# A pair's first products and tanh issued one pair ahead in the mixing of a graph layer

## The chip, the cores and the metric

The kernel runs on one core of a Trainium2 chip. The metric is the device time of one execution in microseconds (us). TensorE (PE) multiplies matrices into PSUM, VectorE (DVE) and GpSimd (POOL) do elementwise work, ScalarE (ACT) does activations such as tanh, and SyncE (SP) issues most of the transfers. The engines run side by side and wait for each other by semaphores; each takes its own instructions in order.

## The reference

The network has four graph layers over 8 batches of 2048 nodes with 64 features. Each layer is `x = x + layer(relu(layernorm(x)))`. The change lies in the end of layer 0, which mixes two candidates per node, `industry` (a product with the adjacency matrix) and `g` (from the hyperedges):

```
def attn_scores(f):
    return jnp.tanh(f @ fcW + fcb) @ av
...
pair = jnp.stack([industry, g], axis=2)
coefs2 = jax.nn.softmax(attn_scores(pair), axis=-1)
out = jnp.einsum('bnk,bnkf->bnf', coefs2, pair)
```

A softmax over two values needs only the difference of the two scores, and the weight of one is half of one plus the tanh of half that difference. The kernel uses this: with d the difference of the two scores, the mix is half of `(industry + g) + (industry - g) * tanh(d / 2)`.

## The kernel before, in words

Features lie on the partitions. Two batches of 64 features fill the 128 partitions, so the 8 batches are 4 pairs, numbered q = 0 to 3. The 2048 nodes are cut in 4 chunks of 512. The function `mix` loops over the chunks and in each over the pairs, 16 turns in all. In the text a pair is named by its q, and a mark as in 0' means the chunk after.

One turn of the loop, for a pair of a chunk:

- For each of the two sources, `ind` and then `g`: two half products with the weights `fcw`, one for each batch (64 partitions each), into a PSUM tile `p1` of two banks (two such tiles exist), and one tanh on ACT over both halves (L658). A tile counts as two half products; each shows as two records in the trace. The trace writes `p` for p1.
- `dt` on POOL is the difference of the two tanh (L660), with two buffers.
- Two products with `av` on PE turn dt into the score `pd`, one PSUM bank. Its tanh, `t2`, is on ACT (L668).
- `total` on POOL is the sum of the two sources (L666).
- On DVE come the mixing operations: `df` = ind - g (L670), times t2 (L671), plus total (L672), and half of it added to `x` (L673).

After the four pairs of a chunk, x is stored (L241), and the layer norm of the next layer is made for that chunk by a generator, `norm_parts`. Its first part centres x on PE (`center`), squares on ACT (L264), takes the relu on ACT or DVE (L269, L267), sums the squares by a product (`to_rows`), and makes the standard deviation: a square root on ACT (L272) and a reciprocal on DVE (L273). Its second part spreads the result by four products (`from_rows`), one for each pair, and DVE multiplies and writes it into two tiles for each pair (L634). These PSUM banks are the three of `bank`. The two parts run at the end of the turns q = 0 and q = 1 of the following chunk. ACT loads a table for the square root and another one for the return to tanh.

At the end of the turn q = 2, `each` brings the next chunk's `g`: four gathers by index on POOL's queue (L750), four tiles of four transposes on PE through `bank` (L756), and copies shared between ACT and DVE (L172, L174).

The order of the code is not the order of the engines. When the program is built, a planner places the instructions of each engine, and the pools decide with their buffers what has to wait. So the trace shows products of the next pair ahead of pd of a pair, although the code names them after it.

Of the kernel before, what the change touches and what calls it, by code (L numbers as in the profile page):

```python
# [7 lines left out]
F = mybir.dt.float32  # L8
# [4 lines left out]
AF = mybir.ActivationFunctionType  # L13
# [6 lines left out]
P = 128  # L20
NB = 8
N = 2048
D = 64
NP = NB // 2
NT = N // P
R = P // NP
CW = 512
NC = N // CW
# [99 lines left out]
class Kernel:  # L128
# [490 lines left out]
    def mix(self, slots, ind, g, fcw, av, each=None):  # L619


        nc, tc = self.nc, self.tc
        big = [slots.tile([P, 2, NP, CW], F, name=f"mix{i}", tag=f"q{6 + i}") for i in range(3)]
        ring = slots.tile([P, 4, 2, CW], F, name="tanh", tag="q9")

        end = [slots.tile([P, 2, NP, CW], F, name=f"end{i}", tag=f"q{4 + i}") for i in range(2)]
        end = end[0][:, 0], end[0][:, 1], end[1][:, 0]
        xe, xo = self.chebyshev(slots)

        def write(q, ch, xr, scale):  # L630
            s = slice(ch * CW, (ch + 1) * CW)
            for i, dst in enumerate((xe, xo)):
                h = slice(i * D, (i + 1) * D)
                nc.vector.tensor_mul(dst(q)[h, s], xr[h], scale[h])  # L634


        with (
            tc.tile_pool(reuse_waits="tile", name="mix", bufs=2) as w,
            tc.tile_pool(reuse_waits="tile", name="mix_ps", bufs=1, space=PSUM) as ps,
        ):  # L640
            def bank():
                return ps.tile([P, CW], F, name="bank", bufs=3)

            norm = iter(())
            if each is not None:
                each(0, bank)
            for ch in range(NC):
                s = slice(ch * CW, (ch + 1) * CW)
                x, sq, xr = end if ch == NC - 1 else (b[:, ch % 2] for b in big)
                nc.sync.dma_start(x, self.xs[0][ch])  # L650
                for q in range(NP):
                    th = [ring[:, 2 * (q % 2) + i] for i in range(2)]
                    for i, src in enumerate((ind, g)):
                        p1 = ps.tile([P, 2, CW], F, name="p1", bufs=2)
                        for half in range(2):
                            h = slice(half * D, (half + 1) * D)
                            self.mm(p1[:, half], fcw[h], src(q)[h, s])
                        nc.scalar.activation(th[i], p1, AF.Tanh, bias=self.col("fcb"))  # L658
                    dt = w.tile([P, 2, CW], F, name="dt")
                    nc.gpsimd.tensor_sub(dt, th[0], th[1])  # L660
                    pd = ps.tile([P, CW], F, name="pd")
                    for half in range(2):
                        self.mm(pd[half * D : (half + 1) * D], av[:, :D], dt[:, half])

                    total = w.tile([P, CW], F, name="total")
                    nc.gpsimd.tensor_add(total, ind(q)[:, s], g(q)[:, s])  # L666
                    t2 = w.tile([P, CW], F, name="t2")
                    nc.scalar.activation(t2, pd, AF.Tanh, scale=0.5)  # L668
                    df = w.tile([P, CW], F, name="df")
                    nc.vector.tensor_sub(df, ind(q)[:, s], g(q)[:, s])  # L670
                    nc.vector.tensor_mul(df, df, t2)  # L671
                    nc.vector.tensor_add(df, df, total)  # L672
                    nc.vector.scalar_tensor_tensor(  # L673
                        x[:, q], df, 0.5, x[:, q], op0=OP.mult, op1=OP.add
                    )
                    if q < 2:
                        next(norm, None)
                    elif q == 2 and each is not None and ch + 1 < NC:
                        each(ch + 1, bank)
                self.store_x(0, ch, x)  # L680
                std = w.tile([P, CW], F, name="std")
                norm = self.norm_parts(ch, x, xr, sq, std, bank, write)
            for _ in norm:
                pass
# [1037 lines left out]
    def attend(self, ih, b, tiles, w, ps, num, den, h1, rows, ed, ed2, shift):  # L1722


        nc, ident = self.nc, self.ident
        HALF = N // 2
        q, s = b // 2, b % 2
        pe = ps.tile([P, HALF], F, name="pe")
        for c in range(2):
            self.mm(  # L1730
                pe[:, c * CW : (c + 1) * CW],
                ident[: 2 * NB, b : b + 1].to_broadcast([2 * NB, P]),
                rows[:, ih * HALF + c * CW : ih * HALF + (c + 1) * CW],
            )
        es = w.tile([P, HALF], F, name="es")
        nc.scalar.copy(es, pe)
        acc = ps.tile([P, HALF], F, name="acc")
        for jt in range(NT):
            m = w.tile([P, HALF], F, name="m", bufs=5)
            e = ed[:, jt, b : b + 1]  # L1740

            t = w.tile([P, HALF], F, name="t")
            nc.gpsimd.tensor_scalar(t, es, 0.2, ed2[:, jt, b : b + 1], op0=OP.mult, op1=OP.add)
            nc.vector.scalar_tensor_tensor(m, es, e, t, op0=OP.add, op1=OP.max)
            nc.vector.tensor_mul(m, m, tiles[jt])
            nc.scalar.activation(m, m, AF.Exp, bias=shift[:, b : b + 1])
            for c in range(2):
                self.mm(
                    acc[:, c * CW : (c + 1) * CW],
                    h1[:, jt, q, s * D : s * D + P], m[:, c * CW : (c + 1) * CW],  # L1750
                    start=jt == 0, stop=jt == NT - 1,
                )
        own, other = slice(s * D, (s + 1) * D), slice((1 - s) * D, (2 - s) * D)
        nc.scalar.copy(num[own], acc[own])
        nc.scalar.copy(den[own], acc[other])
# [595 lines left out]
```

## Time and profile before

| | us |
|---|---|
| median of 3 runs | 2163.15 |
| lowest and highest | 2158.54, 2169.57 |
| the profiled execution, its own time | 2161.53 |
| its span | 2159.8 |
| first tanh of the mixing, L658 | starts at 467.9 |
| last L673 | starts at 617.3 |
| reciprocals of the four norms, L273 | start at 513.76, 553.86, 592.46, 623.49 |
| 32 tanh, L658 | 1.11 each |
| 16 dt, L660 | 2.34 to 2.80 each |
| 16 total, L666 | 1.26 to 1.77 each |
| 16 t2, L668 | 0.60 each |
| 16 L670 | 0.68 to 3.12 each |

The span is the time from the first to the last instruction of the profiled execution; its own time has 1.73 us around it. Positions on the time axis count from the start of the span. In the lines of the page and of the tables by stretches, an engine is followed by its busy time and, after an x, the number of its instructions. In the list of waits stand the engine and the line that waited, what it waited for, the total of it, how often, and the longest one. In the timeline stand the start, the duration, the engine, the line and the operation, and in brackets the idle time before it with what ended it. All products of the helper `mm` have the line L166 and are told apart by their tiles. PE counts as busy also when its clock is low.

### The profile page before, as it was taken

How to read it: one execution, taken by the hardware profiler on the slowest of the kernel's cores; microseconds unless marked ns; L12 is line 12 of the kernel's file. 1: busy time of each engine (PE TensorE's matmuls, PEld its weight loads, DVE VectorE, ACT ScalarE, POOL GpSimd, SP SyncE). 2: the span in 40 equal slices, each digit the busy share in tenths (PEclk: the TensorE clock that was granted, in tenths of full speed). 3: DMA queues.
4: the chain of work that ended last, by engine and by line, in shares of the span. 5: the costliest groups of instructions: out<-in, count | busy, mean ns of one | idle time of the engine just before them, and what ended most of it. 6: DMA issues, size and time to landing. Idle time of an engine off the chain costs nothing. (4 is left out here: it accounts for less than half of the span.)

```text
span 2159.8 us, 21301 instructions
## 1 busy us (share of the span) xinstructions
PE 1945.0 (90%) x7466; PEld 1163.0 (54%) x7466; DVE 1133.9 (53%) x1956; ACT 712.2 (33%) x1343; POOL 706.0 (33%) x595
## 2 busy tenths in 40 slices
PE   5879999978879999999999998899999999669885
PEld 1425766642237774353453543677777666445433
DVE  7877677736661123425434255698703222248774
ACT  6412555534543440020110201324335333248400
POOL 0000467754310005707447166011000000177870
PEclk8868999987769999999999999999999999879997
DMA  8230333441024460050230500556444444375665
GB/s 318 82 109 6 103 104 116 134 166 39 40 80 126 123 175 31 5 151 1 73 83 0 122 1 28 169 176 223 167 125 129 135 149 147 132 221 166 177 184 183
DMA packets 108796, 253.64 MB, mean 117 GB/s; under 512 B 20912, under 2 KB 21056, under 8 KB 101376
## 3 DMA queue, kind: packets, MB, share of 16 engines
q1 hardware_dynamic: 89264, 181.45, 27.0%
q0 software_dynamic: 17104, 66.47, 10.1%
q10 hardware_dynamic: 2304, 4.20, 0.5%
q8 instruction: 62, 1.02, 0.2%
q14 instruction: 62, 0.51, 0.1%
HBM read 218.30 MB, written 33.78 MB: 117 GB/s over the span
## 5 line engine op out<-in xcount | busy, mean ns | idle before, releaser
L325 ACT CAST adj<-adj_t 128x512 fp32r<-128x512 f32 x384 | 237.4, 619 | 687.2 <-PE pp L166 354.7
L1408 POOL TENSOR_TENSOR acc<-acc,y 128x512 f32<-128x512 f32 x224 | 277.2, 1269 | 449.2 <-DVE y L1403 449.2
L166 PE MATMUL pp<-adj,hi 128*128 128x512 f32 x1280 | 365.6, 405 | 0.1
L166 PE MATMUL pk<-q,w 128*128 128x512 f32 (+1 forms) x1024 | 358.2, 611 | 4.3 <-ACT q L1376 3.0
L166 PE MATMUL pp<-adj,lo 128*128 128x512 f32 x1280 | 358.7, 400 | 0.0
L166 PEld LDWEIGHTS pp<-adj,hi 128*128 128x128 f32 x1280 | 242.1, 191 | 72.4 <-issue 16.0
L166 PEld LDWEIGHTS pp<-adj,lo 128*128 128x128 f32 x1280 | 244.0, 191 | 56.5
L166 PEld LDWEIGHTS pk<-q,w 128*128 128x128 f32 (+1 forms) x1024 | 136.5, 188 | 214.1 <-issue 167.3
L1403 DVE SCALAR_TENSOR_TENSOR y<-pk,bias,q 128x512 f32<-128x512 f32 x224 | 157.7, 746 | 142.0 <-PE pk L166 135.7
L166 PE MATMUL acc<-q,ident 128*128 128x512 f32 x416 | 202.9, 614 | 26.4 <-DVE q L2138 16.5
L2048 POOL DMA_INDIRECT ring<-f_rows,near x121 | 139.7, 1154 | 67.0 <-issue 28.0
L166 PEld LDWEIGHTS acc<-q,ident 128*128 128x128 f32 x416 | 76.7, 194 | 102.4 <-issue 47.2
L2152 POOL IOTA q<- 128x2048 int32 x1 | 1.8, 1834 | 316.5 <-PE p L166 316.5
L166 PE MATMUL pp<-adj,x_ind_hi 128*128 128x512 f32 x256 | 94.7, 486 | 2.2 <-DVE q L738 1.9
L1840 POOL TENSOR_TENSOR q<-q,beta 128x512 f32<-128x512 f32 x57 | 67.9, 1193 | 54.6 <-DVE beta L1816 30.8
L1403 DVE SCALAR_TENSOR_TENSOR acc<-pk,bias,q 128x512 f32<-128x512 f32 x32 | 22.6, 747 | 119.9 <-PE pk L166 119.9
L166 PE MATMUL bank<-std,from_rows 32*128 32x512 f32 x128 | 46.7, 894 | 41.9 <-DVE std L273 33.8
L2119 DVE TENSOR_TENSOR q<-ring,e 128x1024 f32<-128x1024 f32 x58 | 70.1, 1219 | 8.9 <-PE acc L166 8.8
L166 PE MATMUL pp<-adj,x_ind_lo 128*128 128x512 f32 x256 | 71.7, 399 | 0.0
L1530 POOL DMA_INDIRECT q<-in_adj_dram,order x15 | 19.0, 1270 | 160.3 <-DVE top L1544 133.5
L166 PEld LDWEIGHTS pp<-adj,x_ind_hi 128*128 128x128 f32 x256 | 48.5, 189 | 38.9 <-issue 23.7
L1495 DVE SCALAR_TENSOR_TENSOR q<-p,cols,q 128x512 f32<-128x512 f32 x16 | 12.0, 751 | 108.4 <-PE p L166 107.5
(411 smaller groups left out, 2768.4 us busy)
## 6 DMA issues: line engine op xcount, KB each, us to landing
adj_t<-in_adjT_dram SPq DMA_DIRECT2D x128, 512.0 KB, 4.0
adj_t<-in_adjT_dram SPq DMA_DIRECT2D x128, 256.0 KB, 3.3
rows<-in_adj_dram SPq DMA_DIRECT2D x16, 1024.0 KB, 5.6
q<-x SPq DMA_DIRECT2D x10, 1024.0 KB, 4.9
x<-q SPq DMA_DIRECT2D x9, 1024.0 KB, 3.9
q<-in_embT_dram SPq DMA_DIRECT2D x8, 1024.0 KB, 11.5
x_ch<-in_xT_dram SPq DMA_DIRECT2D x4, 1024.0 KB, 6.3
h_rows<-q SPq DMA_DIRECT2D x16, 256.0 KB, 3.6
```

Of the source, the lines that this page charges most:

```text
L166: self.nc.tensor.matmul(out, lhsT, rhs, start=start, stop=stop)
L325: nc.scalar.copy(moving, at[:, i])
L1403: nc.vector.scalar_tensor_tensor(y, pks[b, half], bias[:, b : b + 1], emb[:, b], op0=OP.add, op1=OP.mult,)
L1408: nc.gpsimd.tensor_add(acc, acc, y)
L1495: nc.vector.scalar_tensor_tensor(x[:, q], p2, self.col("b2"), x[:, q], op0=OP.add, op1=OP.add)
L1530: nc.gpsimd.indirect_dma_start(row, None, self.a["adj"], bass.IndirectOffsetOnAxis(ap=order[:, 1, t : t + 1], axis=0),)
L1840: self.nc.gpsimd.tensor_tensor(x, x, by.unsqueeze(2).to_broadcast([P, NB, D]), op=OP.mult)
L2048: self.nc.gpsimd.indirect_dma_start(to, None, self.kern.f_rows[:], bass.IndirectOffsetOnAxis(ap=index, axis=0))
L2119: nc.vector.tensor_tensor(y.rearrange("n i (b f) -> n i b f", b=NB), block[:, i : i + 2, : NB * D].rearrange("n i (b f) -> n i b f", b=NB) ...
L2152: nc.gpsimd.iota(whole, pattern=[[1, N]], base=0, channel_multiplier=0)
```

## The change

The first steps of a turn become a function, `attend`: products, tanh, dt and, now directly behind dt, total. It is called once ahead of the loop for the first pair, and then in each turn for the next pair, before the products of this pair's pd. Gathers, transposes and copies of the next chunk (`each`) move from the end of the turn q = 2 to the start of the turn q = 3, since the first pair of the next chunk is now worked on there. In the changed kernel the lines are L653 (tanh), L655 (dt), L657 (total), L681 (t2), L683 to L686 (the four mixing operations), L761 and L767 (gathers and transposes).

```diff
+            def attend(ch, q):
+                s = slice(ch * CW, (ch + 1) * CW)
+                th = [ring[:, 2 * (q % 2) + i] for i in range(2)]
+                for i, src in enumerate((ind, g)):
+                    p1 = ps.tile([P, 2, CW], F, name="p1", bufs=2)
+                    for half in range(2):
+                        h = slice(half * D, (half + 1) * D)
+                        self.mm(p1[:, half], fcw[h], src(q)[h, s])
+                    nc.scalar.activation(th[i], p1, AF.Tanh, bias=self.col("fcb"))
+                dt = w.tile([P, 2, CW], F, name="dt")
+                nc.gpsimd.tensor_sub(dt, th[0], th[1])
+                total = w.tile([P, CW], F, name="total")
+                nc.gpsimd.tensor_add(total, ind(q)[:, s], g(q)[:, s])
+                return dt, total
...
+            pairs = [(ch, q) for ch in range(NC) for q in range(NP)]
+            ahead = attend(*pairs[0])
             for ch in range(NC):
...
                 for q in range(NP):
-                    th = [ring[:, 2 * (q % 2) + i] for i in range(2)]
-                    for i, src in enumerate((ind, g)):
-                        p1 = ps.tile([P, 2, CW], F, name="p1", bufs=2)
-                        for half in range(2):
-                            h = slice(half * D, (half + 1) * D)
-                            self.mm(p1[:, half], fcw[h], src(q)[h, s])
-                        nc.scalar.activation(th[i], p1, AF.Tanh, bias=self.col("fcb"))
-                    dt = w.tile([P, 2, CW], F, name="dt")
-                    nc.gpsimd.tensor_sub(dt, th[0], th[1])
+                    dt, total = ahead
+                    if q == NP - 1 and each is not None and ch + 1 < NC:
+                        each(ch + 1, bank)
+                    if (ch, q) != pairs[-1]:
+                        ahead = attend(*pairs[NP * ch + q + 1])
                     pd = ps.tile([P, CW], F, name="pd")
                     for half in range(2):
                         self.mm(pd[half * D : (half + 1) * D], av[:, :D], dt[:, half])
 
-                    total = w.tile([P, CW], F, name="total")
-                    nc.gpsimd.tensor_add(total, ind(q)[:, s], g(q)[:, s])
                     t2 = w.tile([P, CW], F, name="t2")
...
                     if q < 2:
                         next(norm, None)
-                    elif q == 2 and each is not None and ch + 1 < NC:
-                        each(ch + 1, bank)
```

## The prediction

> **What bounds the kernel now.** The page comes first: TensorE leads, but its share is an average over stages.
>
> ```profile
> PE 1945.0 (90%) x7466; PEld 1163.0 (54%) x7466; DVE 1133.9 (53%) x1956; ACT 712.2 (33%) x1343; POOL 706.0 (33%) x595
> ```
>
> The chain that ended last names 1% of the span, so the mixing is read by itself. Its landmarks are the four reciprocals (L273) at 513.76, 553.86, 592.46 and 623.49 us. The table by stretches between them (PE, PEld, DVE, ACT, POOL, clock, DMA share, GB/s):
>
> ```profile
> 513.76:553.86 40.10, 35.53 (x90) 11.02 (x88) 27.18 (x32) 19.16 (x26) 15.76 (x8) 0.70 0.09 36
> 553.86:592.46 38.60, 33.51 (x90) 10.71 (x88) 27.19 (x33) 19.08 (x26) 15.51 (x8) 0.73 0.07 28
> 592.46:623.49 31.03, 22.98 (x54) 5.89 (x52) 17.49 (x22) 14.58 (x18) 9.21 (x7) 0.72 0.14 44
> ```
>
> DVE, ACT and POOL work 15 to 27 us of 40. PE's 35 us are at a clock of 0.70: at full clock I estimate 18 (16 half products 6.9 with twins side by side, pd 3.4, centring 3.4, to_rows and from_rows 2.0, 16 transposes 2.7). Transfers are nearly absent. So no engine is full: a chunk is a chain of waits. Who waits for whom, 473.7 to 623.5 us:
>
> ```profile
> POOL total L666 <- DVE df L672: 41.0, 9, 7.2
> ACT t L668 <- PE pd L166: 38.3, 16, 5.7
> POOL dt L660 <- ACT tanh L658: 37.6, 14, 4.5
> DVE df L671 <- ACT t L668: 37.5, 16, 8.4
> ```
>
> The last three are one loop: tanh, difference, score, tanh of half the score, mix. Each engine waits some 37 us in it. The timeline of one turn:
>
> ```profile
> 537.34 2.76 POOL L660 TENSOR_TENSOR dt<-tanh 128x1024 f32<-128x1024 f32 x1
> 537.94 2.72 DVE L670 TENSOR_TENSOR df<-q,q 128x512 f32<-128x512 f32 x1
> 540.16 1.14 PE L166 MATMUL pd<-dt,av 128*64 128x512 f32 x4 [1.78 <-POOL dt L660]
> 541.23 2.07 PE L166 MATMUL p<-q,fcw 64*128 64x512 f32 x2
> 541.36 0.60 ACT L668 ACTIVATE t<-pd 128x512 f32<-128x512 f32 x1 [3.16 <-PE pd L166]
> 543.40 1.11 ACT L658 ACTIVATE tanh<-p,cols 128x1024 f32<-128x1024 f32 x1 [1.44 <-PE p L166]
> 544.65 2.35 POOL L660 TENSOR_TENSOR dt<-tanh 128x1024 f32<-128x1024 f32 x1 [4.55 <-ACT tanh L658]
> ```
>
> PE's pd stands ahead of the last half product of the **next** pair, so the next tanh, and with it the next dt, cannot start before this dt has ended: 7.3 us from dt to dt. In the instruction order as built, three of the next pair's four products are ahead of pd already. The change moves the fourth.
>
> **What the Trainium skill says.**
> - "TensorE: Matmul & The Clock Gate", Part 1: the array runs at half or full clock, set by its activity in free-running windows of some 3.4 us. The trace agrees: a centring record is 0.43 us (504.54 to 504.97) or 0.85 (544.24 to 545.10), and the clock drops at 517.1 and 541.2, 7.06 windows apart.
> - "SBUF — State Buffer", Who interferes with whom: a VectorE operation with two SBUF inputs and a GpSimd one that reads SBUF exclude each other. It agrees: L670 at 537.94 takes 2.72 us, 0.69 alone.
> - "TensorEngine Tiling (Array Packing)", Key Properties: tiles on different rows run independently. It agrees: both halves of a p1 (4 records, 515.91) take 1.13 us, one half alone (502.95) 1.12. At half clock: 2.08 and 2.07.
>
> **The change, step by step.** Nothing is added or removed: 64 half products, 32 tanh, 16 dt, 16 total are issued as before. Costed at nothing: the gathers (L750), all 16 issued by 477.2 us and at the same place in POOL's order; the loads and stores of x, in the same order on SP; everything past the mixing, in the same order on every engine. That a later start there carries over one to one is my assumption. Moved: (a) the fourth half product to its twin's side; (b) on ACT, t2 of a pair behind **both** tanh of the next, a new wait; L671 to L673 queue behind it on DVE; (c) total directly behind its dt on POOL; its 41.0 us of waiting were no one's loss; (d) from_rows of q=3 ahead of the last half product of pair 3 and of pd of pair 2: a new wait on PE.
>
> For (b) to (d) I lay out one chunk at **full clock**, from the start of pd of pair 2 (T=0), with 0', 1', ... the next chunk's pairs. Durations: tanh 1.11, t2 0.60, dt 2.35, total 1.27, DVE operations 0.69 (0.1 between dependent ones), reciprocal 3.34, table load 1.28; p1 to its tanh 1.24, pd to t2 1.13 (501.94 to 503.07); four transposes 0.7, one after another; DVE and POOL exclude each other and take turns.
> - Tanh of (3,g) 0.2 to 1.3, t2(2) to 1.9; dt(3) 1.35 to 3.7. DVE ends the last norm's writes at 2.2, waits for the dt; mixing and copies run to 8.1.
> - PE: pd to 1.0, 12 transposes to 3.1, half of p1(0',ind) to 4.1; the fourth tile waits for a bank until 4.75, ends 5.5; the other half to 6.5, p1(0',g) to 7.4, pd(3) to 8.4.
> - Tanh(0',g) 7.75 to 8.85, t2(3) to 9.45. dt(0') 8.9 to 11.25; L671(3) 11.8; total(0') 13.1; L672(3) 13.65; dt(1') 16.0; L673(3) **16.6**.
> - DVE, behind total(1'): L670(1') 18.4, L671 and L672(0'), relu, L673(0'), relu, L670(2') to 22.7, reciprocal to **26.05** (PE and ACT have std ready at 20.95).
> - ACT: second table load to 22.25, tanh(2') to 24.4, t2(1') to 25.0. dt(2') 24.45 to 26.8, L671(1') 27.4, total(2') 28.6, L672(1') 29.2, first write, L673(1'), second write **31.3**: q=0 frees its bank, from_rows q=3 to 32.35, last half product to **33.4**, pd(2').
>
> So the period is 33.4 us at full clock, where the trace has 39.35 (mean of 40.10 and 38.60). **At half clock** the PE steps on that path cost more: 4.05 up to tanh(0',g) (pd 0.9, transposes and halves the rest), 1.9 at tanh(2'), 1.8 at the last two: **41.2**. Between them: PE stands from some 27 to 31, so T=0 finds it at half clock; pd and 12 transposes then fill a window, as the full products from 476.16 did (at full clock by 481.14). I take 0.9 for the first section and 1.8 for the last: **36.1**.
>
> First chunk: tanh(1,g) is free from tanh(0,g) at 470.8, where it had waited for pd(0); PE is continuously busy from 476.16, so clocked up: pd(2) at 484.9 (before: 492.68), reciprocal 22.7 later, 507.6 against 513.76: **-6.2**. Two chunks between: 2 x (36.1 - 39.35) = **-6.5**. End: from reciprocal 10.7 to pd(14), then 14.2 to the last one through L673(15), centring, square, to_rows, std: 24.9, and 4.1 for half clock: 29.0 against 31.03: **-2.0**. Sum **-14.7**: own time 2161.53 to 2146.8. The median of the runs is 1.6 above the profiled time, 2163.15: 2148.5, rounded to **2149**.
>
> Bounds of the unseen. Clock: all half gives start 0, 2 x (41.2 - 39.35) = +3.7, end -0.4: **+3.3**; all full gives -6.2, -11.9, -6.1: **-24**. Taking turns at the shared port: if DVE held it through L671 to L673, L673(3) ends near 14.4, but the reciprocal still ends near 26, as DVE's own list is full there: 0; if each chunk lost one more dt, +2.35 a chunk.
>
> **Rivals.**
> - *Nothing to measure*: the planner had done three quarters, and t2 behind two tanh and two table loads gives the rest back. For it: the bounds touch zero, and DVE, 27.2 of 39 us, is near full in my layout. Against: in 7.3 us from dt to dt the fourth half product is in plain sight. All steady chunks at half clock and the start's -6.2 kept: -6.2 + 3.7 - 0.4 = -2.9, 2160.
> - *Slower*: the new wait (d). PE stands behind from_rows q=3 until DVE, itself late by t2(1'), frees a bank; the idle PE stays at half clock through the next chunk, and POOL's earlier dt gets in front of L672(1') once more: 41.2 + 2.35 = 43.6, three times 4.2 over 39.35: +13, **2176**. It decides once the period exceeds 39.35. Against: the same writes took turns with mixing at 519 to 529, and PE still had work.
> - *More*: full clock throughout, -24, **2139**.
>
> **How the numbers follow.** About 0.5% (10.8 us) is what a measurement can tell from no change. The forecast, -14.7 with its own range of -8 to -20: 0.52; nothing to measure 0.27; slower 0.10; more 0.11. Faster: 0.11 and 0.44 of the forecast, 0.55; slower 0.10; same 0.35. Range: from -25, a little past all-full, to +5, past all-half: 2138 to 2168; left out are the slower rival and little else.
>
> **What would show it.** Right: reciprocals at about 507.6 and then some 36 apart; the wait of POOL's dt for tanh halved; every p1 in four-record pairs; t2 waiting on ACT's own order, not for PE; L670 to L673 longer, by waiting for POOL. Wrong: reciprocals 39 or more apart, PE idle for over 5 us before from_rows q=3, a mean clock under 0.7, or a change outside 462 to 640 us.

## The result and the profile after

The changed kernel takes 2153.12 us (median of 5 runs, 2151.85 to 2156.35), the kernel before 2163.15 (5 runs beside them). The ratio is 0.996, with a 95% interval of 0.9937 to 0.9983: some 0.4% less. The interval leaves out 1, so there is a gain, but it is smaller than the 0.5% from which the prediction would have called it one. A second set, of 13 runs, gave 0.9959 (0.9944 to 0.9974). The profiled execution has a span of 2151.4 us, where before it was 2159.8.

The page of the changed kernel, first line of its busy times, and the table by stretches between its reciprocals (span of the stretch, PE, PEld, DVE, ACT, POOL, clock, DMA share, GB/s; the first one is the end of the first chunk):

```profile
PE 1922.1 (89%) x7466; PEld 1155.0 (54%) x7466; DVE 1149.4 (53%) x1956; ACT 710.8 (33%) x1343; POOL 709.6 (33%) x595
```

```profile
475.50:514.25 38.75, 29.07 (x92) 9.73 (x92) 27.73 (x27) 18.06 (x26) 24.31 (x12) 0.87 0.17 60
514.25:553.23 38.98, 30.47 (x86) 10.34 (x86) 31.06 (x32) 18.62 (x25) 16.34 (x8) 0.78 0.10 40
553.23:591.11 37.88, 29.64 (x92) 9.69 (x89) 30.54 (x31) 18.64 (x25) 16.41 (x8) 0.86 0.07 28
591.11:618.89 27.78, 20.09 (x50) 4.68 (x46) 19.30 (x22) 12.47 (x16) 7.47 (x6) 0.82 0.15 49
```

PE does the same work of a chunk in 4 to 5 us less, and its clock is 0.78 to 0.86 and no longer 0.70 to 0.73. Some 2.6 us of this lie in the products for pd and for the banks, whose number did not change, which points to the clock; the rest lies in p1, where the clock and the placing of the halves both changed. DVE is busy 3 to 4 us **more** in a chunk, with the same instructions. The periods hardly moved: 38.98 and 37.88 us, where they were 40.10 and 38.60.

From the first tanh to the last reciprocal the mixing takes 149.46 us (469.43 to 618.89), and took 155.55 (467.94 to 623.49). This difference of -6.1 splits into -1.0 up to the first reciprocal, -1.8 over the two periods and -3.3 in the end. Outside the mixing the span differs by +1.5 before it begins and -3.8 after it ends (1532.5 us against 1536.3). The instructions there stand in the same order. In four profiles of one set below, which differ in the mixing alone, the part after it lasts from 1549.0 to 1564.2 us, so differences of this size are scatter for a single profile. But in ten of the eleven runs of the changed kernel and its variants the ratio gains more than the mixing does, by up to 9 us; whether something after the mixing gains as well was not looked into. All comparisons below use this length of the mixing beside the ratio.

Who waits for whom in the changed kernel, 475 to 615 us (total, how often, longest):

```profile
POOL dt L655 <- ACT tanh L653: 45.6, 9, 9.0
ACT tanh L653 <- PE p L166: 32.7, 12, 8.5
DVE df L684 <- ACT t L681: 23.9, 10, 8.4
POOL total L657 <- DVE df L685: 15.7, 11, 1.4
ACT t L681 <- PE pd L166: 11.3, 8, 5.3
PE bank L166 <- DVE q L634: 10.8, 3, 3.6
PE bank L166 <- DVE mix L267: 8.1, 3, 3.0
```

The loop of the view before has come apart: t2 waits 11.3 us for pd and no longer 38.3, the multiply by t2 23.9 and no longer 37.5. New are the last two rows: three times PE cannot start a from_rows before a write of the norm (L634) has freed a bank, and three times it cannot start a centring before a relu (L267) has. The first of these is also behind the second row: the wait of tanh for its products has grown from 24.3 to 32.7 us, and three of its waits, of 8.4 to 8.5 us each, end after such a from_rows.

The timeline of one turn and of the norm behind it, changed kernel:

```profile
537.50 2.35 POOL L655 TENSOR_TENSOR dt<-tanh 128x1024 f32<-128x1024 f32 x1 [1.66 <-ACT tanh L653]
537.87 2.52 DVE L684 TENSOR_TENSOR df<-df,t 128x512 f32<-128x512 f32 x1 [0.89 <-ACT t L681]
538.17 2.12 ACT L653 ACTIVATE tanh<-p,cols 128x1024 f32<-128x1024 f32 x2 [0.33 <-PE p L166]
539.90 1.08 PE L166 MATMUL pd<-dt,av 128*64 128x512 f32 x4 [0.98 <-POOL dt L655]
...
541.26 1.77 POOL L657 TENSOR_TENSOR total<-q,q 128x512 f32<-128x512 f32 x1 [1.42 <-DVE df L685]
...
543.00 2.79 POOL L655 TENSOR_TENSOR dt<-tanh 128x1024 f32<-128x1024 f32 x1
543.51 2.83 DVE L684 TENSOR_TENSOR df<-df,t 128x512 f32<-128x512 f32 x1
546.44 0.69 DVE L685 TENSOR_TENSOR df<-df,total 128x512 f32<-128x512 f32 x1
547.05 0.69 DVE L267 TENSOR_SCALAR mix<-bank 128x512 f32<-128x512 f32 x1
547.79 2.08 PE L166 MATMUL bank<-mix,center 128*128 128x512 f32 x2 [2.99 <-DVE mix L267]
549.91 0.60 ACT L264 ACTIVATE mix<-bank 128x512 f32<-128x512 f32 x1 [5.41 <-PE bank L166]
553.23 3.35 DVE L273 RECIPROCAL std<-std 128x512 f32<-128x512 f32 x1 [3.00 <-ACT std L272]
```

From dt to dt it is 5.5 us here (537.50 to 543.00), where the turn shown of before took 7.3: this part of the change works. But now the multiply by t2 on DVE runs beside a dt in 15 of the 16 turns, and then it ends 0.54 to 0.56 us after the dt does, however early it began. At 543.51 the relu stands behind that multiply in DVE's order, the last centring waits for the relu's bank, the square for the centring, and at the end DVE itself waits 3.00 us for its own relu's consequence, the standard deviation.

All 16 multiplies before (L671) and in the changed kernel (L684), shortest, median and longest in ns:

```profile
L671 DVE TENSOR_TENSOR df<-df,t x16: 691/693/694, 478.8 to 615.8; 128x512 f32<-128x512 f32 x16
L684 DVE TENSOR_TENSOR df<-df,t x16: 687/2514/2833, 480.5 to 611.7; 128x512 f32<-128x512 f32 x16
```

Before, all 16 took 0.69 us. Now 15 of the 16 take 1.4 us or more, and together they take 35.5 us, some 24 more than 16 times 0.69. DVE's whole time in the mixing rose by less, 17.2 us (94.2 to 111.4), since other operations are stretched less than before: the 16 of ind - g took 23.4 us before and take 19.8 now.

### The profile page after: what moved, and what is told of

Its sections match the earlier page's. It is cut to its first block, busy times and chain, and to the rows that moved or that the text cites. A ratio compares the mean times of both kernels' runs of the same rounds, so it can differ in the third digit from the quotient of the medians.

```text
span 2151.4 us, 21322 instructions
## 1 busy us (share of the span) xinstructions
PE 1922.1 (89%) x7466; PEld 1155.0 (54%) x7466; DVE 1149.4 (53%) x1956; ACT 710.8 (33%) x1343; POOL 709.6 (33%) x595
```

## The experiments

Each ratio is to the kernel before, run in turn on the same chip. The median of the kernel before itself was from 2163 to 2181 us in different sets, so times are compared by ratio only. "Mixing" is the length from the first tanh to the last reciprocal in the profiled execution: 155.55 us before, 149.46 changed. Edits are on the changed kernel unless the name says before.

**after_again**: the changed kernel once more.

> The changed kernel once more, beside these: the mixing at 149.5 plus or minus 1 us; the ratio to the kernel before again 0.995 to 0.998, though the times on this chip lie some 15 us higher.

Measured: 0.9959 (0.9944 to 0.9974), mixing 150.4. Two profiles of one kernel lie 1 us apart in the mixing, all of it in the first chunk; differences of that size below mean nothing. The times did not lie higher: the kernel before took 2163.23 us here.

**total3**: does total, which waits for its buffer ahead of dt on POOL, cost anything?

```diff
-                total = w.tile([P, CW], F, name="total")
+                total = w.tile([P, CW], F, name="total", bufs=3)
```

> Third buffer for total, everything else as in the changed kernel. In its trace POOL computes total of a pair ahead of that pair's dt, and total waits for L685 of two pairs before (15.7 us in 11 waits), so dt waits behind it. Theory 'POOL order' (dt held behind total, which waits for DVE): those waits go, dt of the second pair of a chunk starts some 2 us earlier, and the mixing, 149.5 us from the first tanh to the last reciprocal, becomes 144 to 147. Theory 'port' (L684 waits for a dt that is running, 2.5 us in place of 0.7): an earlier dt only moves the collision; 149 plus or minus 1. Theory 'bank' (PE waits behind from_rows of the fourth pair): 149 plus or minus 1.

Measured: 0.9969 (0.9944 to 0.9994), mixing 150.7. The wait of total for L685 is gone, and POOL's dt waits for tanh instead:

```profile
POOL dt L655 <- ACT tanh L653: 53.1, 9, 9.0
```

The mixing is no shorter, so these 15.7 us were slack.

**total_back**: total's two lines moved out of `attend`, back behind pd as before the change.

> The changed kernel with total computed where it was before, behind pd, instead of directly behind dt: part (c) of the change undone. Theory 'port': POOL and DVE meet as often, only in another order; mixing 147 to 151. Theory 'POOL order': total no longer stands ahead of the next dt; mixing 143 to 147.

Measured: 0.996 (0.9939 to 0.998), mixing 147.6. Two us less in the mixing, nothing in the times: the place of total in the code isn't what holds the kernel up either.

**no_total**: total removed, by another form of the mix that gives the same value from `df`, `t2` and `g`, with four DVE operations as before.

```diff
-                total = w.tile([P, CW], F, name="total")
-                nc.gpsimd.tensor_add(total, ind(q)[:, s], g(q)[:, s])
...
-                    nc.vector.tensor_mul(df, df, t2)
-                    nc.vector.tensor_add(df, df, total)
+                    nc.vector.scalar_tensor_tensor(df, t2, 1.0, df, op0=OP.add, op1=OP.mult)
                     nc.vector.scalar_tensor_tensor(
-                        x[:, q], df, 0.5, x[:, q], op0=OP.mult, op1=OP.add
+                        df, df, 0.5, g(q)[:, s], op0=OP.mult, op1=OP.add
                     )
+                    nc.vector.tensor_add(x[:, q], x[:, q], df)
```

> total is left out: with s = t2 + 1 the mix is g + (ind - g) * s / 2, which needs four DVE operations as before and nothing on POOL but dt. Theory 'POOL order' and theory 'port' both: 16 operations of 1.27 us leave the shared port, dt never waits for DVE; mixing 149.5 to 141 to 145. L684 still collides with dt (median stays near 2.5). Theory 'bank': PE's wait behind from_rows stays at 3.6 us a chunk and the period near 38; mixing 148 to 150.

Measured: 0.9932 (0.9913 to 0.995), mixing 143.5. POOL without total (16 of 1.26 us and more) gives 6 us, although total's wait for its buffer was slack. The difference ind - g now meets no operation of POOL:

```profile
L681 DVE TENSOR_TENSOR df<-q,q x16: 679/684/693, 468.0 to 603.2; 128x512 f32<-128x512 f32 x16
```

In the changed kernel it took up to 3.36 us. That DVE no longer runs into total fits the gain, but it isn't shown to be its cause. Of the 6 us, 3.7 lie in the first chunk, and the two periods stay at 37.8 and 37.7, near the 38 that theory 'bank' had named.

**norm_late**: the second part of the norm, with from_rows and the writes L634, one turn later, to test whether PE's wait of 3.60 us behind from_rows is what the gain went into.

```diff
-                    if q < 2:
+                    if q in (0, 2):
```

> The second part of the norm (from_rows and the eight writes) moves from the end of the turn q=1 to the end of q=2. Theory 'bank': in the changed kernel PE stands 3.6 us behind from_rows of the fourth pair and then runs the last half product of the pair at half clock, so tanh waits 8.5 us for it, three times; with the part later, the fourth pair's products come first and each of the three periods shrinks by 3 to 5 us: mixing 136 to 142. Theories 'port' and 'POOL order': the eight writes (5.5 us of DVE) only move to another place, where the copies of the next chunk stand behind them; mixing 147 to 151.

Measured: 0.9989 (0.9967 to 1.0012), mixing 154.4, above what any theory had named. The edit did not take away what it was to take away. The wait behind from_rows stayed, and its longest rose from 3.6 to 5.3 us. The norm's second part also meets the gathers' transposes now, and POOL waits for their copies:

```profile
PE bank L166 <- DVE q L634: 12.8, 4, 5.3
POOL total L657 <- ACT q L172: 28.0, 3, 13.2
```

So this place is worse, and what the wait behind from_rows costs in the changed kernel stays untested.

**psum_t2**: the tanh writes the score's own PSUM bank, so that the multiply by t2 has one input in SBUF and one in PSUM.

```diff
-                    t2 = w.tile([P, CW], F, name="t2")
+                    t2 = pd
```

> t2 is written over pd in PSUM in place of SBUF, so L684 has one SBUF input and one in PSUM. Theory 'port': L684 falls from a median of 2.51 us to about 0.7 though a dt runs beside it; total and with it the next dt start some 1.8 us earlier; the mixing goes from 149.5 to 142 to 146, the whole by -4 to -7 us. Theory 'POOL order' agrees with a gain, but a smaller one (-1 to -3), as L685 still waits for the same port. Theory 'bank': no change within 1 us, since PE still waits for DVE's list of eight writes.

Measured: 0.9867 (0.9817 to 0.9917), mixing 129.0, periods 32.08, 33.04 and an end of 26.45. All three theories had expected a far smaller gain. Its multiply (L684) and the addition of total behind it (L685), and then its timeline:

```profile
L684 DVE TENSOR_TENSOR df<-df,pd x16: 673/686/690, 481.0 to 592.3; 128x512 f32<-128x512 f32 x16
L685 DVE TENSOR_TENSOR df<-df,total x16: 679/1645/2055, 481.8 to 593.1; 128x512 f32<-128x512 f32 x16
```

```profile
533.28 2.80 POOL L655 TENSOR_TENSOR dt<-tanh 128x1024 f32<-128x1024 f32 x1
533.78 0.68 DVE L684 TENSOR_TENSOR df<-df,pd 128x512 f32<-128x512 f32 x1
534.38 0.68 DVE L267 TENSOR_SCALAR mix<-bank 128x512 f32<-128x512 f32 x1
535.12 1.12 PE L166 MATMUL bank<-mix,center 128*128 128x512 f32 x2 [0.29 <-DVE mix L267]
```

Under a running dt the multiply takes 0.68 us. The next operation with two SBUF inputs (L685) inherits the stall, but the relu now stands ahead of it, and centring waits 0.29 us where it waited 2.99. The edit did two things at once: it freed the multiply, and the planner placed the relu otherwise. The runs that follow try to separate them.

**before_psum_t2**: the same edit on the kernel before.

> The kernel before with one edit: t2 written over pd in PSUM; the order on every engine is that of the kernel before. Theory 'port': before the change, L671 never met a running dt (all 16 took 0.69 us), so there is nothing to save: the mixing stays at 155.5 plus or minus 1.5 us, and the 20 us that the same edit took off the changed kernel exist only together with the pipelining. Theory 'PSUM is quicker by itself' (shorter t2 or L671): mixing 136 to 148.

Measured: 1.0 (0.9982 to 1.0018), mixing 155.7. The multiply there (L671), with t2 in PSUM:

```profile
L671 DVE TENSOR_TENSOR df<-df,pd x16: 686/687/689, 479.8 to 616.7; 128x512 f32<-128x512 f32 x16
```

It was 0.69 with t2 in SBUF as well. Without the pipelining this multiply had no collision to avoid.

**act_relu**: the relus that DVE did (L267) on ACT, in the mixing alone (`self.mixing` is True from ahead of its loop to behind it). The collisions stay.

```diff
-            if self.flip:
+            if self.flip and not self.mixing:
```

> In the changed kernel's mixing, all four relu of a norm go to ACT, where two of them were on DVE behind L685; nothing else changes. Theory 'relu': centring of the fourth pair waited 2 to 3 us for a bank that such a relu frees (three times), and the edit with t2 in PSUM gained by moving that relu ahead in the order: mixing 149.5 to 140 to 145. Theory 'port' alone: the port collision of L684 stays (median 2.5 us) and sets DVE's list; mixing 147 to 150.

Measured: 0.9877 (0.9814 to 0.9939), mixing 137.5, periods 34.79 and 34.10. Its lines have moved by one or two: L686 is the multiply, L274 the reciprocal.

```profile
L686 DVE TENSOR_TENSOR df<-df,t x16: 693/2516/2850, 478.2 to 597.6; 128x512 f32<-128x512 f32 x16
```

```profile
535.67 3.70 PE L167 MATMUL bank<-mix,center 128*128 128x512 f32 x8
538.28 2.85 DVE L686 TENSOR_TENSOR df<-df,t 128x512 f32<-128x512 f32 x1
544.25 3.34 DVE L274 RECIPROCAL std<-std 128x512 f32<-128x512 f32 x1
```

The multiply still takes 2.5 us, and yet the mixing is 12 us shorter than in the changed kernel: in the norm shown all eight centring records run without a gap, beside the stalled multiply, and the reciprocal has nothing to wait for. So a good part of the loss does not need the multiply to be freed, only that no relu is caught behind it. The 12 us are more than the relu's waits, which were 2 to 3 us a norm. The edit also takes the time of two relus, 1.4 us a chunk, off DVE, and the planner placed PE's centring otherwise; the shares were not separated.

**before_act_relu**: the same edit on the kernel before.

> The kernel before with all relu of the mixing on ACT. Theory 'relu is a wait that the pipelining made': before, a relu that frees a bank stood ahead of L671 and PE did not wait for it; mixing 155.5 plus or minus 1.5 us. Theory 'DVE was short already': 148 to 152.

Measured: 1.001 (0.9996 to 1.0024), mixing 155.8. There, taking the relus off DVE brings nothing. The loss that it avoids arose with the change.

**psum_act_relu**: both edits.

> The changed kernel with both edits, t2 in PSUM and all relu of the mixing on ACT. Alone they brought the mixing from 149.5 to 129.0 and 137.5 us. In the first, DVE's order differed from that of the changed kernel: a relu stood ahead of L685. Theory 'two causes' (the relu's place some 12 us, the port some 8): the relu is already counted in the 129.0, so both together give 126 to 130. Theory 'independent' (t2 in PSUM is worth 20 by the port alone): 115 to 120.

Measured: 0.9897 (0.9867 to 0.9928), mixing 137.3. A miss: I had expected at most 130, and together they are no better than act_relu alone, 8 us worse than psum_t2 alone. The planner's order differs again between the three. Beside psum_t2, 3.7 of the 8 us lie in the second period (36.72 against 33.04), where the granted clock was 0.77 and not 0.85. Which difference in the order does this was not settled.

**psum_no_total**: psum_t2 and no_total together, and the two steps after the tanh written over pd as well, so that of the mixing operations only ind - g has two SBUF inputs.

```diff
-                    t2 = w.tile([P, CW], F, name="t2")
+                    t2 = pd
...
-                    nc.vector.tensor_mul(df, df, t2)
-                    nc.vector.tensor_add(df, df, total)
+                    nc.vector.scalar_tensor_tensor(pd, pd, 1.0, df, op0=OP.add, op1=OP.mult)
                     nc.vector.scalar_tensor_tensor(
-                        x[:, q], df, 0.5, x[:, q], op0=OP.mult, op1=OP.add
+                        pd, pd, 0.5, g(q)[:, s], op0=OP.mult, op1=OP.add
                     )
+                    nc.vector.tensor_add(x[:, q], x[:, q], pd)
```

> The changed kernel with both: t2, and the two mixing steps after it, written over pd in PSUM, and total left out (g is added on DVE). Of DVE's mixing operations only ind - g still has two inputs in SBUF. Theory 'port': the operations take 0.7 us each beside a running dt; mixing 122 to 128, against 129.0 with t2 in PSUM alone; the whole 2125 to 2140 where the kernel before has 2160. Theory 'bank' (DVE's eight writes and PE behind from_rows are what is left): 127 to 131, since they are untouched, and pd is held longer, so its own single bank may become a new wait.

Measured: 0.9802 (0.9743 to 0.986), mixing 120.4, less than was expected and the shortest of all versions. Its multiply:

```profile
L682 DVE SCALAR_TENSOR_TENSOR pd<-pd,df x16: 699/700/700, 476.6 to 580.5; 128x512 f32<-128x512 f32 x16
```

**psum_no_total_act_relu**: the same with the relus on ACT.

> t2 and the steps after it in PSUM, no total, all relu of the mixing on ACT, all upon the changed kernel. Theory 'bank' (what is left is PE behind from_rows of the fourth pair, and DVE's writes): DVE loses 1.4 us a chunk, mixing 117 to 120 where it was 120.4; the whole within 4 us of 2141. Theory 'ACT full': ACT gains 1.2 us a chunk in the stretch where t2 and tanh wait for it; 120 to 123.

Measured: 0.9851 (0.9827 to 0.9874), mixing 122.6. Moving the relus brings nothing here, but it can't be said that it costs: the first chunk, the first period and the end are within 1 us of psum_no_total's, and the loss lies in the second period alone (34.10 against 30.75), where the granted clock was 0.80 and not 0.89. The two intervals overlap, so which of these two is better isn't settled. Against act_relu, which has the relus on ACT too, the mixing is 15 us shorter: with no relu caught, the collisions and total still cost that much together.

## Why the prediction was right or wrong

**Right in range and in kind, by some luck in the number.** The measured 2153.12 us lies inside the stated range and 4 us from the forecast. The forecast was -14.7; the medians of the runs differ by -10.0, the profiled spans by -8.4 and the mixing, where all of it should have come from, by -6.1 alone. So the total looks better than the layout was, by 2.3 us that lie outside the mixing. The sign "reciprocals 39 or more apart" was missed by a hair: they are 38.98 apart, and 39.00 in after_again.

No pd stands between the two halves of a p1 any more, as forecast, but the sign "every p1 in four-record pairs" did not come: nine of the 32 tiles are still split, by transposes, from_rows or centring; the layout itself had two of these splits in a chunk. The tanh t2 waits for ACT's order and little for pd; the clock rose; what changed lies in the mixing. The layout of the first half of a chunk holds: tanh(0',g) was to come 8.65 us after pd of pair 2 at the clock chosen, and came at 8.7 (527.50 to 536.2). The collisions of DVE with dt were in the layout too (L671 of pair 3 waits for dt(0') there), and the Trainium skill's "SBUF — State Buffer", Who interferes with whom, gives both halves of what the runs showed: two SBUF inputs stall (2.51 us), at most one does not (0.686 in psum_t2).

**The turn that was read for all.** "Three of the next pair's four products are ahead of pd already" holds for the turn shown there, but not for every turn. In the two steady chunks of before, three half products of the next pair stand ahead in one turn of four, two in two turns, and none in the turn q=0:

```profile
586.89 1.08 PE L166 MATMUL pd<-dt,av 128*64 128x512 f32 x4
587.90 1.12 PE L166 MATMUL bank<-mix,center 128*128 128x512 f32 x2
588.95 1.80 PE L166 MATMUL bank<-mix,to_rows 128*32 128x512 f32 x8
590.68 1.99 PE L166 MATMUL p<-q,fcw 64*128 64x512 f32 x8
```

Here all four (eight records) come after pd. In the changed kernel all four are ahead in every turn. The change moved more than "the fourth"; the numbers did not suffer, since they were laid out from the changed order.

**The step that failed: "PE and ACT have std ready at 20.95".** The layout let DVE's own list set the reciprocal at 22.7, and 23.6 with the clock. The list itself was near: counted back from 22.7 in steps of 0.69, its relus lie at 19.9 and 21.3, or 0.9 later with the clock, and in the trace they start 19.55 and 21.46 after pd(2) (547.05 and 548.96). But the bank that the first of these relus frees is needed by the last centring, and then come square, to_rows and standard deviation. In the trace that takes from 547.05 to 552.51, 5.5 us, of which about 1 us is half clock: the two centring records took 2.08 us here, and 1.12 in psum_t2. From the layout's own relu at 19.9 the standard deviation could thus not start before some 24 (an estimate from these figures), and in the trace it starts at 25.0. A reciprocal at 22.7 was ruled out by that relu; I had put relus into DVE's list without asking who waits for them. The term from pd(2) to the reciprocal was 25.7 in this chunk, 2.1 more than laid out. act_relu fits this: with that dependency off DVE the periods are 34.8 and 34.1, below the forecast of 36.1. They fall by more than these 2.1 us, so act_relu does not measure this term alone.

**The start, -6.2, was -1.0.** pd(2) came at 487.37, near the 484.9 laid out plus the 1.5 by which the mixing began later. From there to the reciprocal it was 26.9 us and not 22.7. The timeline of the changed kernel:

```profile
488.74 1.78 POOL L657 TENSOR_TENSOR total<-q,q 128x512 f32<-128x512 f32 x1 [1.42 <-DVE df L685]
490.47 2.79 POOL L655 TENSOR_TENSOR dt<-tanh 128x1024 f32<-128x1024 f32 x1
490.99 2.82 DVE L684 TENSOR_TENSOR df<-df,t 128x512 f32<-128x512 f32 x1
493.73 0.41 DVE L174 COPY q<-bank 128x256 f32<-128x256 f32 x1
494.20 0.66 PE L767 MATMUL bank<-ident,q 128*128 128x128 f32 x4 [3.24 <-DVE q L174]
```

It is the same fault in another place: the multiply stalls under dt, a copy (L174) stands behind it, and the last tile of transposes waits 3.24 us for the copy's bank. Then comes the relu's wait as in every chunk (2.15 us in this one). In the layout this tile waited only until 4.75 after pd(2), and here until 6.8.

**The two periods, -6.5, were -1.8.** Of the 2.9 us by which 38.98 exceeds 36.1, 2.1 are the relu's above. The other 0.75 are from the reciprocal to pd(2'): 13.25 us, laid out as 12.5 with its half clock. In the second period, 37.88, the split is another. The part up to pd(2) took 13.9, 1.4 more than laid out. The part after it ran nearly at full clock, with tanh(0',g) 7.8 after pd(2), and still took 24.0, where the layout has 22.7 at that clock. The new wait (d) came as named, there and in both other chunks, but at the size of a few us:

```profile
523.53 2.04 PE L166 MATMUL bank<-std,from_rows 32*128 32x512 f32 x2 [3.60 <-DVE q L634]
525.50 2.07 PE L166 MATMUL p<-q,fcw 64*128 64x512 f32 x2
527.50 1.97 PE L166 MATMUL pd<-dt,av 128*64 128x512 f32 x4
527.67 1.11 ACT L653 ACTIVATE tanh<-p,cols 128x1024 f32<-128x1024 f32 x1 [8.54 <-PE p L166]
```

Each of the first three takes what the layout gives it at half clock; the excess lies ahead of them, as from_rows starts 9.3 us after the reciprocal (10.0 in the next chunk) and not 8.6.

**The end, -2.0, was -3.3**: 27.78 us, forecast 29.0. The 24.9 laid out at full clock needed 2.9 of the 4.1 added for half clock.

**Minor steps.** "Total directly behind its dt" was wrong in order: the planner put the next pair's total ahead of its dt on POOL, where it waits for its buffer. total3 shows that at nothing. "The wait of POOL's dt for tanh halved" was wrong: it rose from 37.6 to 45.6 us, since a faster turn only lets POOL come sooner to the norm's gap (there it waits 7.1, 9.0 and 8.1 us); it was a poor sign to watch. The second drop of the clock, read as 541.2, lies at about 541.06 (the granted clock is 0.64 from 541.0 to 541.2, 1.00 before and 0.50 after), so the two drops are 23.9 us apart, 7.0 of the prediction's windows. The rivals with numbers: "nothing to measure" (-2.9) is nearer than the forecast to the -6.1 of the mixing, and the forecast is nearer to the -10.0 of the medians; its mechanism, steady chunks at half clock, did not come. "Slower" by wait (d) fell, as the periods stayed under 39.35. "More" (-24) needed full clock throughout, and the clock was 0.78 to 0.87. psum_t2 and psum_no_total gain that and more in the mixing, but with edits that the rival did not have.

**What stays open.** That the pipelining made collisions, and that they and what is caught behind them cost most of the gain, is shown: psum_t2 and act_relu each shorten the changed kernel's mixing and leave the kernel before as it was, and psum_no_total, where the collisions are all but gone, ends 35 us below the kernel before (its form without the sum was not tried on that kernel). No run shows how much of this is the relu's wait alone: the planner reordered in each of these runs, act_relu also unloads DVE, and psum_t2 and the relus on ACT do not add up, though each alone brings 12 to 20 us. The granted clock moves along with the mixing (0.78 to 0.87 in the changed kernel, 0.81 to 0.94 in psum_no_total), and how much of each gain comes through it was not separated. What the wait behind from_rows costs is untested.

## What to carry to other kernels

When a change makes two engines overlap, list for every operation that will be stretched what stands **behind it in the same engine's order** and who waits for that. A short operation that frees a bank, caught behind a stall, can cost more than its own length shows. In a layout by hand, each operation put into an engine's list needs its consumer's earliest time checked against what is written further down. And if two engines exclude each other on SBUF inputs, moving one operand into the PSUM bank where its input lies anyway costs one line: here the pipelining with it brought 1.3%, and 2.0% with the sum dropped and its steps rewritten too, where the pipelining alone brought 0.4%. It has to be tried together with the pipelining: on the kernel before, it brought nothing.

## What the runs showed of the hardware that was not expected

- A stall can move on: with the multiply freed in psum_t2 (0.686 us), the next operation with two SBUF inputs (L685) takes 1.645 us in the median, where it took 0.692 in the changed kernel. In psum_no_total, with one such operation left in the mixing and no total, that one took at most 1.19 us.
- A whole dt passes through: the multiply that began 0.5 us after a dt of 2.79 us took 2.83 (543.00 and 543.51 us), ending 0.55 us after it. The dt itself is 2.34 to 2.35 us in 11 of 16, and 2.79 to 2.80 in the five that began while ind - g was running on DVE.
- From 523.5 to 527.5 us PE was busy without a gap, in from_rows on 32 rows and half products on 64 rows, and stayed at half clock (2.04 and 2.07 us for two records each); the granted clock rose between 532 and 533 us, after pd and 12 transposes, and the two p1 tiles from 536.93 (eight records in 1.99 us) were at full clock. Before, PE stayed at half clock from 519.4 to 534 us with hardly a gap, in products of 32, 64 and 128 rows, so being busy for a few us was not enough there. Whether the rows in use decide this was not tested.
